# Inner products read from ScalarE's copy, r3 ahead of r7, and the next layer's statistics and logits rearranged in a two-layer graph kernel

## The chip, the cores and the metric

The kernel runs on one core of one Trainium2 chip. The metric is the device time of one execution in microseconds (us); the median of three runs is given. One further execution was taken with the hardware profiler, and every duration below that has a place in the timeline comes from it. PE is TensorE (matrix products), ACT is ScalarE, DVE is VectorE, POOL is GpSimd, and SP issues the DMAs.

## The reference

Sixteen batches of x (1024 nodes by 512 features) pass through two residual layers with one adjacency matrix adj (1024 by 1024). All is float32.

```python
# layer 0
h = relu(layernorm(x))
x = x + (adj @ h) @ W0 + bias
# layer 1
h = relu(layernorm(x))
u = h @ W                              # 512 x 512
s1, s2 = u @ a1, u @ a2                # one number per node each
e = leaky_relu(s1[:, :, None] + s2[:, None, :], 0.2) * adj
att = softmax(e, axis=2)
x = x + elu(att @ u + beta * u)
```

In the kernel, u is the name of the normalized and rectified input of layer 1 (the reference's second h), so that s1 = u . (W a1) and s2 = u . (W a2): two dot products per node with vectors v that are worked out once. These dot products are called the logits.

## The kernel before

**Products.** Each large product of a batch is done as seven half-size products and sums (Strassen's scheme in Winograd's form). Layer 0's adj @ h has p1, p2, p6, p5, p7, p3 and p4, in that order. Their results are added up in PSUM banks Y, W and X (two banks each, p = 0 and 1) and read from there into C11, C12, C22, C21 and the sums S1, S2, S4, in SBUF. Its product with W0 (`po`) has seven products again. Layer 1 has the products `z` (attention by u) and `pq` (by W).

**The second level.** For batches 1 to 15 the function `products_a2` (line 215) takes each of p1 to p4 apart once more: `inner_steps(prod)` returns seven inner products r1 to r7 as steps. An inner product is two matmul calls, which are four records in the trace. r1, r6 and r7 are accumulated in a PSUM tile that the product has for itself, `yx` (its left half is y; the right half, x, is used where the bank isn't being started): r1 writes y, ScalarE copies that value to `t[:, 0]`; r6 adds to y, VectorE adds that and `t5` (ScalarE's copy of r5) into `t[:, 1]`; r7 adds to y again, ScalarE copies it to `t[:, 2]`. Then VectorE adds `t[:, 0:2]` to bank 1 behind r3, and what r7 gave to bank 0. The pool of `yx` has two buffers, so p6 takes that of p1, p5 that of p2, p7 that of p6, and so on: a product's r1 waits until all readers of y of the product two before it are done. Names in the trace: `y_p1y` is y of p1, `y_p1t` is its t, `in_p` are the sums of parts of h that a product's inner products take as inputs, `y_Y`, `y_W` and `y_X` are the banks, `y_C` the blocks C, `y_S` the sums and also the scratch tile for statistics.

Two products are interleaved (p1 with p2, p6 with p5, p7 with p3), two inner products to a numbered step; p4 is interleaved with the first product by W0. Steps 0 to 6 are p1 and p2, 7 to 13 p6 and p5, 14 to 20 p7 and p3, 21 to 27 p4. `reads` folds a finished bank into its blocks C.

**The side work.** After each numbered step, `after(k)` issues the work that a plan has put there. All engines keep the order in which the program issues their instructions (the wrapper at line 118 sees to it, which is why every record has that line). There is no scheduler: an instruction that waits holds all that is behind it on its engine.

`plan_out` (line 1093) is such a plan, for the output of layer 0 of the batch before. That output lies in four tiles xr, named by (half, quarter): (0,0), (0,1), (1,0), (1,1), two chunks of 128 nodes each. For each tile: `keep` stores it, `stats` takes the mean and the variance, `relu` normalizes it in place (ScalarE), `logits` takes the dot products with both v (VectorE, two reductions a chunk), `store` writes u to DRAM. `inner_left` makes sums of parts of adj @ h's inputs (VectorE), `load_res` loads the next residual tiles, `begin` puts the bias into a bank.

Statistics have two forms in the class `Norm` (line 454). `sums(k)` works on ScalarE, two passes over a chunk with accumulated sums and one small scaling; the last chunk is followed by three small GpSimd instructions (scale, power -1/2, product) that give `r` and `nb`, the factor and the offset of the relu. `stats()` works on VectorE, one bn_stats and one bn_aggr a chunk, followed by four small GpSimd instructions.

**The last batch.** Batch 15 has no next batch to prepare. In its layer 0 stands the softmax of layer 1's first batch instead: `FIRST_A` (line 1163) and `FIRST_B` (line 1167) say at which step. R reloads a masked row block from DRAM (`er<-ed`, SP) into a buffer of the pool b4 (12 buffers, shared with t, C and the sums), E takes its exponentials (ScalarE, four instructions with accumulated sums), V transposes it (VectorE, two), S and s spread the sums, B and b take the SBUF tiles for the transposed halves, D, d and T divide out the sums on the diagonal and add blocks for the product. Steps of `FIRST_A` lie in steps 0 to 27 of the batch, those of `FIRST_B` in the rest.

```python
order = "r1 r4 r5 r6 r2 r7 r3" if first else "r1 r2 r5 r4 r6 r3 r7"
turns = ones[0:2] + [t for m in range(5) for t in (twos[m], ones[m + 2])] + twos[5:]
for m in range(7):
    turns[2 * m]()
    turns[2 * m + 1]()
    if m == 0:
        for prod, p in behind:
            reads(prod, p)
    elif m in (4, 5):
        reads(one, halves[m - 4])
    after(k + m)
```

Of the kernel before, what the change touches and what calls it, by code (L numbers as in the profile page):

```python
# [65 lines left out]
def kernel(  # L66
# [12 lines left out]
    B, N, D = x.shape  # L79
# [21 lines left out]
    def bank(name):  # L101
        return psum.tile([P, 512], F32, tag="ps", name=name)
# [21 lines left out]
    def add(o, i0, i1, op=ALU.add):  # L124
        dve.tensor_tensor(o, i0, i1, op=op)
# [89 lines left out]
    def products_a2(name, inner, weighted, after, s4):  # L215


        read = ReadA(name, None, s4)
        read.s3_now = False
        banks = {}  # L220
        by_name = {p[0]: (n, *p[1:]) for n, p in enumerate(PRODUCTS)}

        def inner_steps(prod):

            _, an, bn, kind, first, last = by_name[prod]
            left, sums, right, ext = inner[prod]
            if first:
                banks[kind, 0], banks[kind, 1] = bank(f"{name}_{kind}0"), bank(f"{name}_{kind}1")  # L230
            i0, i1 = banks[kind, 0], banks[kind, 1]
            yx = psum_y.tile([P, 512], F32, tag="psy", name=f"{name}_{prod}y")
            y, x = yx[:, 0:256], (i0 if first else yx)[:, 256:512]
            t = b4.tile([P, 4, 256], F32, tag="b4", name=f"{name}_{prod}t")
            t5 = sums[:, 3].rearrange("p c d -> p (c d)")
            lefts = {
                "r1": left[:, 0:2, P : 2 * P], "r2": left[:, 2:4, P : 2 * P],
                "r7": left[:, 0:2, 0:P], "r4": left[:, 2:4, 0:P], "r5": sums[:, 0],
                "r6": sums[:, 1], "r3": sums[:, 2],
            }  # L240
            rights = {
                "r1": right[:, 0:2, 0:256], "r7": right[:, 0:2, 256:512],
                "r2": right[:, 2:4, 0:256], "r3": right[:, 2:4, 256:512],
                "r5": ext[0], "r6": ext[1], "r4": ext[2],
            }
            outs = {
                "r1": (y, True), "r4": (i0[:, 0:256], first), "r5": (x, False),
                "r6": (y, False), "r7": (y, False), "r2": (i1[:, 0:256], first),
                "r3": (i1[:, 256:512], False),
            }  # L250

            def step(r):
                o, start = outs[r]
                for k in range(2):
                    pe.matmul(
                        o, lefts[r][:, k, :], rights[r][:, k, :], start=(start and k == 0),
                        stop=(k == 1), skip_group_check=True,
                    )
                if r == "r1":
                    act.copy(t[:, 0, :], y)  # L260
                elif r == "r5":
                    act.copy(t5, x)
                elif r == "r6":
                    add(t[:, 1, :], y, t5)
                elif r == "r7":
                    act.copy(t[:, 2, :], y)
                    if first:
                        i0v = i0.rearrange("p (a n) -> p a n", a=2)
                        add(i0v, i0v, t[:, 2:3, :].to_broadcast([P, 2, 256]))
                    else:  # L270
                        add(t[:, 3, :], y, t5)
                        add(out(0), i0, t[:, 2:4, :].rearrange("p a n -> p (a n)"))
                elif r == "r3":
                    add(out(1), i1, t[:, 0:2, :].rearrange("p a n -> p (a n)"))

            def out(p):
                return read.block("C21", p) if prod == "p4" else banks[kind, p]

            order = "r1 r4 r5 r6 r2 r7 r3" if first else "r1 r2 r5 r4 r6 r3 r7"
            return [partial(step, r) for r in order.split()]  # L280

        def reads(prod, p):
            read(prod, p, banks[by_name[prod][3], p])

        k = 0
        behind = []
        for one, two in (("p1", "p2"), ("p6", "p5"), ("p7", "p3")):
            ones, twos = inner_steps(one), inner_steps(two)
            halves = (0, 1) if one == "p1" else (1, 0)
            turns = ones[0:2] + [t for m in range(5) for t in (twos[m], ones[m + 2])] + twos[5:]  # L290
            for m in range(7):
                turns[2 * m]()
                turns[2 * m + 1]()
                if m == 0:
                    for prod, p in behind:
                        reads(prod, p)
                elif m in (4, 5):
                    reads(one, halves[m - 4])
                after(k + m)
            behind = [(two, p) for p in ((1, 0) if two == "p3" else (0, 1))]  # L300
            k += 7
        inn = inner_steps("p4")
        steps = iter(weighted.steps(0, read.c["C11"]))
        for m in range(7):
            inn[m]()
# [3 lines that stand above are left out]
            elif m > 4:  # L309
                read.last(6 - m)  # L310
            next(steps)()
            if m == 3:
                next(steps)()
            elif m == 6:
                read.s3(0)
                read.s3(1)
            after(k + m)
        return read.left()

    class Weighted:  # L320
# [17 lines left out]
        def steps(self, n, left):  # L338

            prod, _, bn, kind, first, last = self.products[n]  # L340
            first = first and (kind, 0) not in self.banks

            def step(q, i, dc):
                if first and i == 0 and dc == 0:
                    self.banks[kind, q] = bank(f"{self.name}_{kind}{q}")
                ps = self.banks[kind, q].rearrange("p (i o) -> p i o", i=2)
                pe.matmul(
                    ps[:, i, :], left[:, dc, ts(2 * q + i, P)], self.w[:, W_BLOCK[bn], dc, :],
                    start=(first and i == 0 and dc == 0), stop=(last and dc == 1),
                    skip_group_check=True,  # L350
                )
                if i and dc:
                    self.done(prod, q, ps)

            return [partial(step, q, i, dc) for q in range(2) for i in range(2) for dc in range(2)]
# [93 lines left out]
    def stats(mv, src):  # L449
        st = stat.tile([P, 6], F32, tag="bn", name="bn")  # L450
        dve.bn_stats(st, src)
        dve.bn_aggr(mv, st)
# [145 lines left out]
    def junk(k):  # L598

        return junks[-1][:, k, :]  # L600
# [7 lines left out]
    class LayerOut:  # L608
# [17 lines left out]
            xr = xrs[self.b, nh, q]  # L626
            sp.dma_start(out=x1d[self.b][nh, q], in_=xr.rearrange("p k d -> p (k d)"))

        def stats(self, nh, q, k):
            xr = xrs[self.b, nh, q]  # L630
            if k == 0:
                self.us[nh, q] = xr
                self.norms[nh, q] = Norm(f"u{self.b}_{nh}_{q}", xr, junk(0))
            self.norms[nh, q].sums(k)

        def relu(self, nh, q):
            self.norms[nh, q].relu()
# [378 lines left out]
    halves = [(nh, q) for nh in range(2) for q in range(2)]  # L1016
# [76 lines left out]
    def plan_out(o, b):  # L1093

        return steps(
            (-1, o.keep, 0, 1), (-1, o.keep, 1, 0), (-1, o.keep, 1, 1), (0, o.stats, 0, 1, 0),
            (1, o.relu, 0, 0), (2, o.stats, 1, 0, 0), (3, o.stats, 1, 0, 1),
            (4, o.stats, 0, 1, 1), (6, o.relu, 1, 0), (7, o.relu, 0, 1), (8, o.stats, 1, 1, 0),
            (9, o.stats, 1, 1, 1), (11, o.relu, 1, 1),
            (3, o.store, 0, 0), (7, o.store, 1, 0), (8, o.store, 0, 1), (13, o.store, 1, 1),  # L1100
            (2, o.logits, 0, 0, 0), (3, o.logits, 0, 0, 1), (7, o.logits, 1, 0, 0),
            (8, o.logits, 1, 0, 1), (9, o.logits, 0, 1, 0), (10, inner_left, b, "p7"),
            (11, o.logits, 0, 1, 1), (12, inner_left, b, "p3"), (13, o.logits, 1, 1, 0),
            (14, o.logits, 1, 1, 1), (15, inner_left, b, "p4"), (16, o.store_logits),
            (18, begin, b, "Y"), (24, begin, b, "X"),
            (9, load_res, b, 0, 0), (12, load_res, b, 0, 1), (15, load_res, b, 1, 0),
            (18, load_res, b, 1, 1),
        )

# [15 lines left out]
    def plan_softmax(order, s):  # L1125
# [35 lines left out]
        13: {9: "N n"},  # L1161
    }
    FIRST_A = {
        13: "R0", 15: "B E0", 16: "V0 R1", 17: "E1", 18: "V1 R2", 19: "E2", 20: "V2 b", 21: "R3",
        23: "E3", 24: "V3 R4 S", 25: "E4", 26: "V4 R5",
    }
    FIRST_B = {
        2: "E5 R6", 3: "V5 E6 R7", 4: "V6", 5: "E7", 6: "V7 s D", 7: "T1a", 8: "T1b", 11: "d T2a",
        12: "T2b",
    }  # L1170
    LOADS_U = {5: ("U00",), 7: ("U01",), 9: ("U10", "U11")}

# [115 lines left out]
```

## Time and profile before

| | |
|---|---|
| median of three runs | 2312.18 us (2311.99 to 2313.05) |
| profiled execution | 2311.76 us |
| its span, first to last instruction | 2310.0 us |
| mean granted TensorE clock | 0.996 |
| chain that ended last, by engine | PE 56%, DVE 21%, ACT 13%, DMA 4%, issue 4% |
| layer 0 of one batch: batches 1 to 5 | 68.76 us |
| batches 6 to 14 | 69.31 us |
| batch 15 | 81.35 us |
| layer 1 of one batch | 72.24 us |

The lengths of batches are taken from the start of one batch's first p1 record to the next one's, and in layer 1 from `z` to `z`. A record of the timeline reads: start in us from the span's start, length in us, engine, line, operation, output <- inputs, size, number of neighbouring records of the same kind drawn together, and in brackets how long the engine stood idle ahead of it and whose end let it go on. In the list of waits, a row names the waiting instruction, the one waited for, and the total in us, the number of times and the longest.

### The profile page before, as it was taken

To read this page: it belongs to the slowest core of one execution; us is meant where nothing else is said; L and a number is where in the kernel's file an instruction comes from. 1 tells how busy PE (TensorE), PEld (TensorE's weight loads), DVE (VectorE), ACT (ScalarE), POOL (GpSimd) and SP (SyncE) were. 2 spreads that over 40 slices of the span, in tenths; PEclk is the share of its full clock that TensorE was granted. 3 is DMA by queue.
4 is the path that set the end of the run, shared out by engine and by line. 5 is a ranking of instruction groups with operands and counts; after the bars stand their busy time and mean duration, and the time that the engine had idled before them with its cause. 6 is when DMAs were issued, how large, how long until landed. Compare 5 with 4: busy or idle time off the path is not lost.

```text
span 2310.0 us, 29805 instructions
## 1 busy us (share of the span) xinstructions
PE 2262.2 (98%) x8524; PEld 1608.5 (70%) x8524; DVE 1894.6 (82%) x4225; ACT 1585.9 (69%) x4256; POOL 372.1 (16%) x553
## 2 busy tenths in 40 slices
PE   9999999999999999999899999999999999999998
PEld 5788888888888888888665566655665556655565
DVE  7888888888888888888788888888887888878774
ACT  3776777776777776776466677677776777767753
POOL 1111111111111111111011222112221122201220
PEclk9999999999999999999999999999999999999999
DMA  7333454433444433343545544554446543455441
GB/s 216 126 128 124 142 167 129 143 122 128 139 156 137 141 124 128 120 146 123 191 133 166 161 136 164 189 170 150 144 161 195 169 133 125 142 184 165 132 129 37
DMA packets 194294, 336.04 MB, mean 145 GB/s; under 512 B 78801, under 2 KB 86993, under 8 KB 194129
## 3 DMA queue, kind: packets, MB, share of 16 engines
q1 hardware_dynamic: 193808, 333.61, 44.4%
q8 instruction: 67, 1.10, 0.2%
q14 instruction: 99, 0.80, 0.1%
q10 hardware_dynamic: 320, 0.52, 0.1%
HBM read 228.33 MB, written 109.91 MB: 146 GB/s over the span
## 4 chain that ended last, share of the span: by engine, by line
PE 56%; DVE 21%; ACT 13%; DMA 4%; issue 4%; SPq 1%; POOL 1%; DVEq 0%; ACTq 0%
PE z_Y L118 14%; PE pq_Y L118 8%; PE z_X L118 7%; ACT y_S L118 5%; PE pq_X L118 4%; PE y_Y L118 4%; PE z_W L118 4%; DVE in_p L118 4%; PE po_Y L118 3%; PE y_X L118 2%; DVE y_S L118 2%; DVE hS L118 2%; PE y_p4y L118 2%; DVE xr L118 2%; PE pq_W L118 2%
## 5 line engine op out<-in xcount | busy, mean ns | idle before, releaser
L118 POOL TENSOR_TENSOR x<-x,r 128x512 f32<-128x512 f32 x120 | 198.7, 1673 | 935.0 <-DVE x L118 325.6
L118 ACT ACTIVATE e<-e,nm 128x256 f32<-128x256 f32 x480 | 237.1, 497 | 140.7 <-DVE nm L118 140.7
L118 DVE CUSTOM_DVE_ANT_0 e<-e,mask 128x256 f32<-128x256 f32 x512 | 215.4, 476 | 106.9 <-DMA mask<-maskd 89.7
L118 PE MATMUL z_Y<-pT,ul_U 128*128 128x512 f32 x512 | 224.9, 592 | 0.0
L118 ACT ACTIVATE e<-s2b,s1b 128x256 f32<-128x256 f32 x512 | 216.4, 500 | 0.0
L118 PE MATMUL po_Y<-w_c,y_C 128*128 128x256 f32 x768 | 189.2, 380 | 1.1 <-DVE xr L118 1.1
L118 PEld LDWEIGHTS z_Y<-pT,ul_U 128*128 128x128 f32 x512 | 97.3, 190 | 115.6 <-issue 108.1
L118 PE MATMUL pq_Y<-w_c,z_C 128*128 128x256 f32 x768 | 174.5, 380 | 0.7 <-ACT z L118 0.6
L118 DVE CUSTOM_DVE_ANT_0 y_S<-xr,v_bc 128x512 f32<-128x512 f32 x240 | 165.3, 689 | 11.5 <-ACT y_S L118 0.5
L118 PEld LDWEIGHTS pq_Y<-w_c,z_C 128*128 128x128 f32 x768 | 145.5, 190 | 28.9 <-issue 7.7
L118 PEld LDWEIGHTS po_Y<-w_c,y_C 128*128 128x128 f32 x768 | 146.0, 191 | 22.7 <-DVE xr L118 2.3
L118 DVE STREAM_TRANSPOSE pT<-e 128x512 f32<-128x512 f32 x240 | 155.5, 686 | 1.0
L118 ACT ACTIVATE y_S<-xr 128x512 f32<-128x512 f32 x120 | 75.8, 631 | 92.3 <-DVE xr L118 91.3
L118 ACT ACTIVATE h<-h,nb_h,r_h 128x512 f32<-128x512 f32 (+1 forms) x132 | 98.2, 792 | 54.5 <-POOL nb_h L118 54.5
L118 PE MATMUL po_X<-w_c,y_S 128*128 128x256 f32 x512 | 115.7, 379 | 0.0
L118 PE MATMUL pq_X<-w_c,z_S 128*128 128x256 f32 x512 | 115.6, 379 | 0.0
L118 PE MATMUL z_Y<-pT_T,ul_U 128*128 128x512 f32 x256 | 113.6, 594 | 1.2 <-DVE pT_T L118 1.1
L118 PE MATMUL z_X<-pT,ul_S 128*128 128x512 f32 x256 | 112.5, 592 | 0.0
L118 PE MATMUL z_Y<-pT_T,ul_S 128*128 128x512 f32 x256 | 112.5, 592 | 0.0
L118 PE MATMUL z_W<-pT,ul_U 128*128 128x512 f32 x256 | 112.5, 592 | 0.0
L118 PE MATMUL z_X<-pT_T,ul_S 128*128 128x512 f32 x256 | 112.5, 592 | 0.0
L118 PEld LDWEIGHTS po_X<-w_c,y_S 128*128 128x128 f32 x512 | 97.3, 190 | 13.2
(231 smaller groups left out, 5113.3 us busy)
## 6 DMA issues: line engine op xcount, KB each, us to landing
mask<-maskd SPq DMA_DIRECT2D x128, 512.0 KB
h<-in_x_dram SPq DMA_DIRECT2D x64, 512.0 KB
xr<-in_x_dram SPq DMA_DIRECT2D x256, 128.0 KB
x1d<-xr SPq DMA_DIRECT2D x64, 512.0 KB
ul_U<-ud_U SPq DMA_DIRECT2D x64, 512.0 KB
x<-x1d SPq DMA_DIRECT2D x64, 512.0 KB
out_dram<-x SPq DMA_DIRECT2D x252, 128.0 KB
ud_U<-xr SPq DMA_DIRECT2D x60, 512.0 KB
```

Of the source, the lines that this page charges most:

```text
L118: return lambda *args, **kwargs: tc.keep_in_program_order(f(*args, **kwargs))
```

## The change

It has six parts. (1) Where a bank isn't being started, VectorE's sum behind r7 takes r7's result from ScalarE's copy `t[:, 2]` and no longer from y in PSUM. (2) The order of inner products of a product that starts its bank (p1, p2, p5) becomes r1 r4 r5 r2 r6 r3 r7. (3) The reads of the first product of a pair move from steps 4 and 5 to steps 5 and 6, bank 1 first, and so stand behind the copies of r7. (4) Statistics of the tile (0,1) are taken with `stats()` on VectorE, at step 0, and no longer with two calls of `sums` at steps 0 and 4. (5) `plan_out` is rearranged: relu(0,0) from step 1 to 0, relu(0,1) from 7 to 2, logits of (0,1) from 9 and 11 to 3 and 4, those of (0,0) from 2 and 3 to 1 and 2, stats of (1,0) and (1,1) one to three steps sooner, sums for p3 and p4 one and three steps later; two stores and two loads move too. (6) The softmax in batch 15 starts with a reload at step -1, and its exponentials E0 to E3 are spread over steps 4 to 23; E4 moves into the rest of the batch.

```diff
--- before.py
+++ after.py
@@ -268,7 +268,7 @@
                         i0v = i0.rearrange("p (a n) -> p a n", a=2)
                         add(i0v, i0v, t[:, 2:3, :].to_broadcast([P, 2, 256]))
                     else:
-                        add(t[:, 3, :], y, t5)
+                        add(t[:, 3, :], t[:, 2, :], t5)
                         add(out(0), i0, t[:, 2:4, :].rearrange("p a n -> p (a n)"))
                 elif r == "r3":
                     add(out(1), i1, t[:, 0:2, :].rearrange("p a n -> p (a n)"))
@@ -276,7 +276,7 @@
             def out(p):
                 return read.block("C21", p) if prod == "p4" else banks[kind, p]
 
-            order = "r1 r4 r5 r6 r2 r7 r3" if first else "r1 r2 r5 r4 r6 r3 r7"
+            order = "r1 r4 r5 r2 r6 r3 r7" if first else "r1 r2 r5 r4 r6 r3 r7"
             return [partial(step, r) for r in order.split()]
 
         def reads(prod, p):
@@ -286,7 +286,6 @@
         behind = []
         for one, two in (("p1", "p2"), ("p6", "p5"), ("p7", "p3")):
             ones, twos = inner_steps(one), inner_steps(two)
-            halves = (0, 1) if one == "p1" else (1, 0)
             turns = ones[0:2] + [t for m in range(5) for t in (twos[m], ones[m + 2])] + twos[5:]
             for m in range(7):
                 turns[2 * m]()
@@ -294,10 +293,10 @@
                 if m == 0:
                     for prod, p in behind:
                         reads(prod, p)
-                elif m in (4, 5):
-                    reads(one, halves[m - 4])
+                elif m > 4:
+                    reads(one, 6 - m)
                 after(k + m)
-            behind = [(two, p) for p in ((1, 0) if two == "p3" else (0, 1))]
+            behind = [(two, 1), (two, 0)]
             k += 7
         inn = inner_steps("p4")
         steps = iter(weighted.steps(0, read.c["C11"]))
@@ -626,12 +625,16 @@
             xr = xrs[self.b, nh, q]
             sp.dma_start(out=x1d[self.b][nh, q], in_=xr.rearrange("p k d -> p (k d)"))
 
-        def stats(self, nh, q, k):
+        def stats(self, nh, q, k=None):
+
             xr = xrs[self.b, nh, q]
-            if k == 0:
+            if not k:
                 self.us[nh, q] = xr
                 self.norms[nh, q] = Norm(f"u{self.b}_{nh}_{q}", xr, junk(0))
-            self.norms[nh, q].sums(k)
+            if k is None:
+                self.norms[nh, q].stats()
+            else:
+                self.norms[nh, q].sums(k)
 
         def relu(self, nh, q):
             self.norms[nh, q].relu()
@@ -1093,17 +1096,16 @@
     def plan_out(o, b):
 
         return steps(
-            (-1, o.keep, 0, 1), (-1, o.keep, 1, 0), (-1, o.keep, 1, 1), (0, o.stats, 0, 1, 0),
-            (1, o.relu, 0, 0), (2, o.stats, 1, 0, 0), (3, o.stats, 1, 0, 1),
-            (4, o.stats, 0, 1, 1), (6, o.relu, 1, 0), (7, o.relu, 0, 1), (8, o.stats, 1, 1, 0),
-            (9, o.stats, 1, 1, 1), (11, o.relu, 1, 1),
-            (3, o.store, 0, 0), (7, o.store, 1, 0), (8, o.store, 0, 1), (13, o.store, 1, 1),
-            (2, o.logits, 0, 0, 0), (3, o.logits, 0, 0, 1), (7, o.logits, 1, 0, 0),
-            (8, o.logits, 1, 0, 1), (9, o.logits, 0, 1, 0), (10, inner_left, b, "p7"),
-            (11, o.logits, 0, 1, 1), (12, inner_left, b, "p3"), (13, o.logits, 1, 1, 0),
-            (14, o.logits, 1, 1, 1), (15, inner_left, b, "p4"), (16, o.store_logits),
+            (-1, o.keep, 0, 1), (-1, o.keep, 1, 0), (-1, o.keep, 1, 1), (0, o.stats, 0, 1),
+            (0, o.relu, 0, 0), (1, o.stats, 1, 0, 0), (2, o.relu, 0, 1), (3, o.stats, 1, 0, 1),
+            (5, o.relu, 1, 0), (6, o.stats, 1, 1, 0), (8, o.stats, 1, 1, 1), (10, o.relu, 1, 1),
+            (1, o.logits, 0, 0, 0), (2, o.logits, 0, 0, 1), (3, o.logits, 0, 1, 0),
+            (4, o.logits, 0, 1, 1), (7, o.logits, 1, 0, 0), (9, o.logits, 1, 0, 1),
+            (10, inner_left, b, "p7"), (13, inner_left, b, "p3"), (15, o.logits, 1, 1, 0),
+            (16, o.logits, 1, 1, 1), (16, o.store_logits), (18, inner_left, b, "p4"),
+            (3, o.store, 0, 0), (5, o.store, 0, 1), (8, o.store, 1, 0), (13, o.store, 1, 1),
             (18, begin, b, "Y"), (24, begin, b, "X"),
-            (9, load_res, b, 0, 0), (12, load_res, b, 0, 1), (15, load_res, b, 1, 0),
+            (8, load_res, b, 0, 0), (10, load_res, b, 0, 1), (14, load_res, b, 1, 0),
             (18, load_res, b, 1, 1),
         )
 
@@ -1161,12 +1163,12 @@
         13: {9: "N n"},
     }
     FIRST_A = {
-        13: "R0", 15: "B E0", 16: "V0 R1", 17: "E1", 18: "V1 R2", 19: "E2", 20: "V2 b", 21: "R3",
-        23: "E3", 24: "V3 R4 S", 25: "E4", 26: "V4 R5",
+        -1: "R0", 4: "E0", 8: "B V0 R1", 10: "E1", 12: "V1 R2", 17: "E2", 18: "V2 R3", 23: "E3",
+        25: "b", 26: "V3 R4 R5",
     }
     FIRST_B = {
-        2: "E5 R6", 3: "V5 E6 R7", 4: "V6", 5: "E7", 6: "V7 s D", 7: "T1a", 8: "T1b", 11: "d T2a",
-        12: "T2b",
+        2: "E4 S R6", 3: "V4 E5 R7", 4: "V5 E6", 5: "D V6 E7", 6: "V7 s", 7: "T1a", 8: "T1b",
+        11: "d T2a", 12: "T2b",
     }
     LOADS_U = {5: ("U00",), 7: ("U01",), 9: ("U10", "U11")}
 
```

## The prediction

> **What bounds the kernel now.** I read, in this order, the share of each engine and of each engine on the chain that ended last, the waits of TensorE, two windows of one batch each, and TensorE's timeline with its idle gaps.
>
> ```profile
> PE 2262.2 (98%) x8524; PEld 1608.5 (70%) x8524; DVE 1894.6 (82%) x4225; ACT 1585.9 (69%) x4256; POOL 372.1 (16%) x553
> ...
> PE y_p7y L118 <- DVE y_p6t L118: 16.7, 15, 1.4
> PE y_p3y L118 <- DVE y_p3t L118: 5.2, 1, 5.2
> PE y_X L118 <- ACT y_C L118: 4.3, 15, 0.3
> PE y_Y L118 <- ACT y_C L118: 3.5, 9, 0.4
> PE y_p4y L118 <- DVE y_p4t L118: 2.1, 1, 2.1
> ```
>
> [...]TensorE is never short of work for long; all that the change can win in the fifteen batches of this stage is in these five rows, about 32 us, and anything it makes late by a microsecond per batch costs about 15. The windows of batch 8 and batch 15 (length, then busy time of PE, PEld, DVE, ACT, POOL):
>
> ```profile
> 573.62:642.93 69.31, 67.55 (x309) 58.10 (x308) 58.48 (x132) 50.98 (x132) 10.20 (x25) 1.00 0.43 138
> 1058.83:1140.18 81.35, 71.57 (x309) 59.80 (x308) 63.01 (x136) 44.60 (x138) 4.67 (x13) 0.96 0.47 155
> ```
>
> [...]No other engine is full, so losses are moments at which one instruction on VectorE or ScalarE stands in a queue while TensorE needs its result. These moments are:
>
> ```profile
> 587.12 1.13 PE L118 MATMUL y_Y<-adjT_T,hS 128*128 128x256 f32 x4 [0.38 <-ACT y_C L118]
> ...
> 599.92 1.13 PE L118 MATMUL y_p7y<-adjT_B,h 128*128 128x256 f32 x4 [1.09 <-DVE y_p6t L118]
> ...
> 603.93 1.13 PE L118 MATMUL y_X<-adjT_B,hS 128*128 128x256 f32 x4 [0.29 <-ACT y_C L118]
> ...
> 1101.84 2.07 PE L118 MATMUL y_p3y<-adjT_B,hS 128*128 128x256 f32 x4 [5.22 <-DVE y_p3t L118]
> ...
> 1116.18 1.13 PE L118 MATMUL y_p4y<-adjT_T,h 128*128 128x256 f32 x4 [2.08 <-DVE y_p4t L118]
> ```
>
> An inner product (four records) takes 0.864 us from start to start, and a wait costs 0.10 more, because the group after it takes 1.13 where others take 1.03. By starts, batch 8 loses 0.65 at y_Y, 0.22 at y_p6y (hidden in its start, 589.06), 1.36 at y_p7y, 0.56 at y_X and 0.05 in p4: 2.84. So a batch with no such loss would take 69.31 - 2.84, about 66.5.
>
> **What the Trainium skill says.** "GPSIMD Engine Reference", section Key points: GpSimd "Shares its SBUF interfaces with VectorE — contention with DVE instructions in a 2-port perf mode or with two SBUF inputs." The trace agrees, and gives the size. Unheld, then beside VectorE's sums of two SBUF tiles:
>
> ```profile
> 583.37 0.19 POOL L118 TENSOR_SCALAR r_u<-mv_u 128x2 f32<-128x2 f32 x1 [6.04 <-ACT y_S L118]
> 583.64 0.70 POOL L118 TENSOR_TENSOR r_u<-r_u,half 128x2 f32<-128x2 f32 x1
> 584.42 0.20 POOL L118 TENSOR_TENSOR nb_u<-mv_u,r_u 128x2 f32<-128x2 f32 x1
> ...
> 632.37 0.74 POOL L118 TENSOR_SCALAR r_h<-mv_h 128x2 f32<-128x2 f32 x1 [5.16 <-ACT y_S L118]
> 633.19 1.02 POOL L118 TENSOR_TENSOR r_h<-r_h,half 128x2 f32<-128x2 f32 x1
> ...
> 632.37 0.69 DVE L118 TENSOR_TENSOR hS<-hS,h 128x512 f32<-128x512 f32 x1
> ```
>
> The 0.19 us step became 0.74: it ended with the sum beside it. I read this as a rule for the working: a GpSimd instruction that meets a two-input VectorE instruction ends no sooner than that one. "TensorE: Matmul & The Clock Gate", Part 1, says that the clock halves after an idle window of about 3.4 us. The trace agrees: the group behind the 5.22 us wait took 2.07, those behind waits of 1 or 2 us 1.13. No other page bears on the argument.
>
> **The change, part by part.** Times t count from the start of p1 in batch 8 (573.62); turn n starts at 0.864 n if nothing waits (turn 11 at 583.12 does). The order that the change gives was laid out engine by engine, with durations from the trace.
>
> *The copies.* r7 reads y from ScalarE's copy, so y is free once the copy is made, and VectorE's add leaves the wait of p7 on p6's y: saves the 1.36. C11's and C12's copies go behind r7's copies, so they no longer hold ScalarE when y is due; r3 in front of r7 gives i1 sooner. Together the y_X, the y_Y and the 1.36 go: about 2.6 of the 2.84. The add costs the same: a sum of 256 columns takes 0.42 with y from PSUM (y_p1t, 579.07) and with both inputs in SBUF (in_p, 575.07). Free by itself.
>
> *Statistics of u(0,1).* ScalarE loses two chunks of 1.84 us each (574.90, 576.87: two passes, two reads, a scaling). VectorE gets bn_stats and bn_aggr twice, 0.79 a chunk start to start by the late chunks of layer 1:
>
> ```profile
> 1278.63 0.68 DVE L118 BATCH_NORM_STATS2 bn<-late 128x6 f32<-128x512 f32 x1
> 1279.35 0.18 DVE L118 BATCH_NORM_AGGREGATE mv_u<-bn 128x2 f32<-128x6 f32 x1
> ```
>
> GpSimd gets four small instructions in place of three (0.27 + 0.78 + 0.27 + 0.20 = 1.52 unheld). These stand at step 0 of p1, on VectorE behind the sums for the next inputs, whose last is issued at 577.81: t = 4.53 to 6.23 for the statistics.
>
> *Logits sooner.* Behind the statistics on VectorE come logits(0,0), four reductions, 2.91 us (579.42 to 582.33 in before), t = 6.11 to 9.02, then p1's r6 add to 9.36, then logits(0,1), which needs relu(0,1), which needs GpSimd's four steps, which start at t = 6.32 — beside logits(0,0), whose reductions each have two SBUF inputs. In flight they are 6.11-6.79, 6.83-7.52, 7.67-8.36 and 8.41-9.10. By the rule above GpSimd's steps end at 6.84, 8.07, 8.41 and 9.15 rather than 7.85. The relu's first half then runs on ScalarE 9.18 to 9.99, logits(0,1) from 10.02: two reductions 1.35, the Y add 0.60, two reductions 1.40, and only then p2's r6 add, from 13.4 to 13.84. That add frees y for p2's r7, in turn 13, planned for 11.23. TensorE resumes at 13.9: a loss of 2.6. Bounds: with GpSimd unheld 13.14, a loss of 1.9 here; with every step held to the end of a reduction begun later, one reduction (0.74) more. I take the middle.
>
> *What is late next.* ScalarE had the relus of 1.52 us in front of p6's copy; now relu(1,0) stands behind a GpSimd chain of the same kind, then C11's copies, p2's copy and 1.71 us of statistics of (1,1) come before p6's first copy, which ends at t = 18.7 to 18.9. p6's r5, turn 17, planned at 14.69, starts at 18.7 to 19.0: both delays together 4.0 to 4.3 with the restarts of 0.10. Then about 0.1 to 0.3 at p3's r7 (behind the four sums for p4, now in step 18) and about 0.2 in p4: 4.6 to 4.9 a batch, against 2.84. Net +1.75 to +2.05; I take +1.9, for each of 14 batches: +26.6.
>
> *Loads and stores.* Two stores change places and the loads of residuals come a step sooner; SP issues them, each in tenths of a microsecond, and what they fetch is used tens of microseconds later. Nothing, unless a buffer comes free later; then SP stands, and load_res with it.
>
> *Batch 15.* It alone has the softmax's exponentials for layer 1 (reload a row block, four exponentials, transposes). In before they are packed into p3 and p4, and each reload waits for a buffer:
>
> ```profile
> 1098.06 0.51 ACT L118 ACTIVATE er<-er,nm 128x256 f32<-128x256 f32 x1 [6.22 <-DMA er<-ed]
> ```
>
> That is where ScalarE stood, p3's add came late, TensorE idled 5.22 and then ran at half clock: 5.39 for the wait, 3.04 for the half clock, 2.34 at y_p4y, and 1.77 at the beginning of the rest of the batch: 12.5 of the 81.35. The change starts the reloads two thirds of a batch sooner, at step -1, one at a time. The buffer is then asked for before the exponentials want it, and I leave the 1.77 at its end, where the last exponentials still stand, as it is: 69.3 + 1.9 + 1.7 = 72.9, so -8.5. Bounds: nothing gained if the sooner reloads hold a buffer that p1 needs (above: 0), and 10.4 gained if the delays of the other batches are absent here (69.3 + 1.7).
>
> Sum: 26.6 - 8.5 = +18.1 on the profiled execution's 2311.76 (span 2310.0 and 1.8 around it): 2329.9. The median of the runs stands 0.4 above it, 2312.18: 2330.
>
> **The rivals.** *GpSimd isn't held by reductions*: the profile shows the hold beside sums, and beside a reduction only once (a GpSimd sum of 512 columns at 1282.97, in layer 1). Then logits(0,1) begins 1.3 sooner, p2's loss is 1.9 or less and ScalarE's chain after it too, a batch costs +0.3 to +0.5, batch 15 gives 10 back: 14 x 0.5 - 10 = -3, 2309. Against it: 632.37. *The other side: the change does what it says.* If p2's r6 add is done by t = 11.2 (the point that decides; it needs logits(0,1) begun by t = 7.4, or that add in front of it), the 2.6 are won, little comes back: -2.3 x 14 - 8.5 = -41, 2271. Against it: relu(0,1) can't start before GpSimd's chain, 7.85 at best. *Batch 15 gives nothing*, since the reload for E0 takes a buffer that the inner sums want and TensorE idles there instead, or ScalarE's lateness reaches one turn further (0.7 a batch): 2338 to 2340; for it, the buffers were the limit before, against it, the reloads are spread.
>
> **How the numbers follow.** Forecast 0.68 (2322 to 2338 by the bounds of +1.4 to +2.4 a batch); GpSimd unheld 0.12, mostly within no change; as intended 0.04; nothing from batch 15, or deeper, 0.12; others 0.04. A measurement of this kernel can tell 0.2%, 4.6 us, from none. Faster 0.08 (as intended, a third of the unheld case), same 0.09, slower 0.83. The range, 2308 to 2342, takes in the unheld case and the worse one.
>
> **What would show it.** Right: among TensorE's waits y_p7y for VectorE and y_X for ScalarE are gone, and new ones stand fifteen times, p2's y for VectorE's p2 copy at 2 to 3 us and p6's y for ScalarE at 1 to 1.5; GpSimd's four steps at p1 take 2.5 to 3 us and not 1.5; a batch takes about 71.2, batch 15 about 73. Wrong: no wait over 1 us in p2, batches under 69, or batch 15 still over 78; the first two say that the logits are hidden, the third that reloads still wait for a buffer.

## The result and the profile after

| | before | after |
|---|---|---|
| median | 2312.09 us (2311.33 to 2313.05, four runs) | 2328.69 us (2326.92 to 2329.89, four runs) |
| profiled execution | 2311.76 us | 2329.89 us |
| its span | 2310.0 us | 2328.1 us |
| layer 0, batches 1 to 5 | 68.76 us | 70.4 to 70.7 us |
| batches 6 to 14 | 69.31 us | 71.1 us |
| batch 15 | 81.35 us | 72.26 us |
| layer 1, all batches | 1169.8 us | 1172.8 us |

The ratio of the runs is 1.0071 (95% interval 1.0054 to 1.0088): slower by 0.7%. Of the 18.1 us between the spans, batches 1 to 14 give +24.5 (from the first p1 of batch 1 to that of batch 15: 967.90 before, 992.36 after), batch 15 gives -9.1, layer 1 gives +3.0 and what lies ahead of batch 1 gives -0.3. Layer 1 has the same instructions in both, and in the thirteen profiled executions of this study it took from 1169.4 to 1175.8 in no visible relation to what was edited, so its 3.0 are not counted as the change's.

TensorE's waits after the change (instruction, what it waits for, total us, times, longest):

```profile
PE y_p2y L118 <- DVE y_p2t L118: 31.9, 15, 2.3
PE y_p6y L118 <- ACT y_p6t L118: 11.7, 9, 1.3
...
PE y_p3y L118 <- DVE y_p3t L118: 1.2, 1, 1.2
```

All five rows shown of before have gone or, for p3, shrunk from 5.2 to 1.2. Two others stand in their place, and they are larger. (The waits named y_Y, z_Y and pq_Y that the full list has besides belong to the start of the kernel and to layer 1.) The windows of batch 8 and batch 15, in the columns used for before:

```profile
585.13:656.30 71.17, 68.86 (x309) 59.34 (x308) 59.96 (x136) 48.38 (x122) 12.66 (x26) 0.98 0.41 134
1083.01:1155.27 72.26, 67.81 (x309) 58.08 (x308) 64.61 (x143) 41.71 (x128) 6.66 (x14) 1.00 0.54 175
```

VectorE is 1.5 us busier in batch 8 and ScalarE 2.6 us less. Neither is near full, and yet the batch is 1.86 us longer: it is a matter of order. The chain can be read in the timeline of batch 8 (which begins at 585.13), here on GpSimd and VectorE:

```profile
591.50 0.54 POOL L118 TENSOR_SCALAR r_u<-mv_u 128x2 f32<-128x2 f32 x1 [2.67 <-DVE mv_u L118]
592.12 1.15 POOL L118 TENSOR_TENSOR r_u<-r_u,half 128x2 f32<-128x2 f32 x1
593.34 0.28 POOL L118 TENSOR_SCALAR nb_u<-mv_u 128x2 f32<-128x2 f32 x1
593.70 0.65 POOL L118 TENSOR_TENSOR nb_u<-nb_u,r_u 128x2 f32<-128x2 f32 x1
...
593.61 0.69 DVE L118 CUSTOM_DVE_ANT_0 y_S<-xr,v_bc 128x512 f32<-128x512 f32 x1
```

The last of the four small steps ends at 594.35, 0.05 us after the reduction of logits(0,0) that started at 593.61 and ended at 594.30; unheld such a step takes 0.20. Then ScalarE, VectorE and TensorE go on from one to the next:

```profile
594.39 1.52 ACT L118 ACTIVATE xr<-xr,nb_u,r_u 128x512 f32<-128x512 f32 x2 [1.84 <-POOL nb_u L118]
...
595.24 0.69 DVE L118 CUSTOM_DVE_ANT_0 y_S<-xr,v_bc 128x512 f32<-128x512 f32 x1 [0.59 <-ACT xr L118]
...
598.53 0.42 DVE L118 TENSOR_TENSOR y_p2t<-y_p2y,in_p 128x256 f32<-128x256 f32 x1
...
599.00 1.15 PE L118 MATMUL y_p2y<-adjT_B,h 128*128 128x256 f32 x4 [2.31 <-DVE y_p2t L118]
```

The brackets say who released whom: GpSimd the relu, the relu the logits of (0,1); the sum at 598.53 has no bracket, because VectorE was not idle. It had merely stood behind these logits, so the list of waits, which names the sum, doesn't name the instructions that made it late.

In batch 15 the waits of 5.2 and 2.1 us are gone. E0 to E3, which are now spread over steps 4 to 23, don't wait for their reloads: the record of E2 has no bracket, where E1 of before has 6.22 us. In before ScalarE waited for a reload five times in this batch, 19.7 us in all; now it does so twice, 3.4 in all, for exponentials in the rest of the batch, and TensorE's list of waits shows no loss from it:

```profile
1118.04 0.51 ACT L118 ACTIVATE er<-er,nm 128x256 f32<-128x256 f32 x1
...
1142.10 0.51 ACT L118 ACTIVATE er<-er,nm 128x256 f32<-128x256 f32 x1 [2.85 <-DMA er<-ed]
```

### The profile page after: what moved, and what is told of

It is laid out like the page before. It is cut to its first block, busy times and chain, and to the rows that moved or that the text cites. A ratio compares the mean times of both kernels' runs of the same rounds, so it can differ in the third digit from the quotient of the medians.

```text
span 2328.1 us, 29746 instructions
## 1 busy us (share of the span) xinstructions
PE 2264.6 (97%) x8524; PEld 1614.1 (69%) x8524; DVE 1916.3 (82%) x4285; ACT 1544.9 (66%) x4106; POOL 408.8 (18%) x568
## 4 chain that ended last, share of the span: by engine, by line
PE 62%; DVE 16%; ACT 10%; DMA 5%; POOL 3%; issue 3%; SPq 1%; DVEq 0%; ACTq 0%; POOLq 0%
PE z_Y L118 13%; PE pq_Y L118 7%; PE z_X L118 6%; PE y_Y L118 6%; PE y_X L118 4%; PE pq_X L118 4%; PE po_Y L118 4%; PE z_W L118 4%; ACT e L118 3%; DVE in_p L118 3%; ACT y_S L118 3%; PE y_p3y L118 2%; DVE xr L118 2%; DVE hS L118 2%; PE y_p4y L118 2%
## 5 line engine op out<-in xcount | busy, mean ns | idle before, releaser
L118 ACT ACTIVATE xr<-xr,nb_u,r_u 128x512 f32<-128x512 f32 x120 | 91.1, 806 | 70.8 <-POOL nb_u L118 70.8
L118 ACT ACTIVATE y_S<-xr 128x512 f32<-128x512 f32 x90 | 56.8, 632 | 91.8 <-DVE xr L118 91.4
```

Source lines behind the costliest of these rows:

```text
L118: return lambda *args, **kwargs: tc.keep_in_program_order(f(*args, **kwargs))
```

## The experiments

Each was timed beside the kernel before, and the ratios are to it. Its median lay between 2312.09 and 2313.83 us in these timings, so that a difference between two of the other kernels is good to about 2 us. Where a stretch at half clock follows a wait in some batches only, the last section says which.

**The logits of (0,1) behind p2's sum.** The changed kernel with

```diff
-(3, o.logits, 0, 1, 0), (4, o.logits, 0, 1, 1),
+(5, o.logits, 0, 1, 0), (6, o.logits, 0, 1, 1),
```

> The changed kernel, with the logits of (0,1) moved from steps 3 and 4 to steps 5 and 6, so that p2's r6 sum stands in front of them on VectorE. Theory M (two queues are late because of the same relu chain: VectorE in front of p2's r7, ScalarE in front of p6's r5, and the second deadline holds the whole delay): the wait of p2 is gone, a wait of p6's y for ScalarE's copy of 3.5 to 4 us takes its place in every batch, a batch stays at 70.3 to 71.1, time 2322 to 2329, or more if TensorE drops to half clock behind so long a gap. Rival R1 (VectorE's queue alone is the loss): p2's 2.3 us come back, a batch takes 68.3 to 68.8, time 2293 to 2298.

Measured: 2337.12 us, ratio 1.010 (1.0085 to 1.0115), 7 to 8 us slower than the changed kernel. TensorE's waits:

```profile
PE y_p6y L118 <- ACT y_p6t L118: 18.4, 14, 1.3
PE y_p5y L118 <- ACT y_p2t L118: 16.7, 14, 1.2
PE y_p6y L118 <- ACT y_p1t L118: 5.6, 11, 2.1
```

The largest wait of the changed kernel is gone and nothing is won: ScalarE's lateness, which it had covered, comes to light in three waits within 7 us. It isn't the one wait of 3.5 to 4 us that was expected, as p2's r7 copy and p1's are late too. Batches 6 to 14 take 70.9 or 72.5 us by turns, and the timeline of one of the longer shows why:

```profile
677.36 1.13 PE L118 MATMUL y_p5y<-adjT_T,hS 128*128 128x256 f32 x4 [1.19 <-ACT y_p2t L118]
...
679.81 2.08 PE L118 MATMUL y_p6y<-ext,in_p 128*128 128x256 f32 x4 [1.31 <-ACT y_p6t L118]
681.67 1.72 PE L118 MATMUL y_X<-ext,hS 128*128 128x256 f32 x4
```

In place of 1.13 and 1.03 us these two groups took 2.08 and 1.72: TensorE ran at half clock for a while, in 7 of the 14 batches. R1 is refuted: even where the clock stayed full, batches took 70.2 and 70.9, not 68.3 to 68.8. Theory M holds, with the half clock that it left open.

**ScalarE's relu and statistics later too.** The same, and

```diff
-(5, o.relu, 1, 0), (6, o.stats, 1, 1, 0), (8, o.stats, 1, 1, 1), (10, o.relu, 1, 1),
+(7, o.relu, 1, 0), (8, o.stats, 1, 1, 0), (9, o.stats, 1, 1, 1), (11, o.relu, 1, 1),
```

> The changed kernel, with the logits of (0,1) at steps 5 and 6 and also ScalarE's relu(1,0) and the statistics of (1,1) two steps later (relu(1,0) 5 to 7, statistics 6 to 8 and 8 to 9, relu(1,1) 10 to 11), so that both queues give way to TensorE's needs. Theory M: both waits shrink, a batch takes 67.8 to 68.5, time 2286 to 2293. R1: no more than the run with the logits alone would give, 2293 to 2298. R2 (the bn statistics on VectorE are the loss): no gain, 2325 to 2330.

Measured: 2285.47 us, ratio 0.9881 (0.9865 to 0.9898); batches of 67.4 (1 to 5) and 68.1 (6 to 14). Both waits have gone from the list. One of the three that the first experiment brought to light is left, and it is that experiment's in number and size:

```profile
PE y_p6y L118 <- ACT y_p1t L118: 5.6, 11, 2.1
```

What the first edit could not win at all, the two together win: some 43 us against the changed kernel. The bn statistics are still on VectorE here, which speaks against R2. This is still 12.5 us more than the changed kernel with the plan of before (below); which of the plan's other moves cost that was not tried apart.

**ScalarE's part alone.** The changed kernel, the logits left at steps 3 and 4, with

```diff
-(5, o.relu, 1, 0), (6, o.stats, 1, 1, 0),
+(6, o.relu, 1, 0), (7, o.stats, 1, 1, 0),
```

> The changed kernel, with relu(1,0) at step 6 in place of 5 and the first statistics of (1,1) at step 7 in place of 6, so that p6's first copy stands in front of them on ScalarE; the logits stay at steps 3 and 4. Theory M: p2's wait of about 2 us stays, the wait of p6's y for ScalarE goes, a batch takes 69.4 to 70.1, time 2308 to 2314. R1 (VectorE's queue alone): nothing, 2326 to 2331.

Measured: 2321.25 us, ratio 1.004 (1.0026 to 1.0055): 7 us won, not 15 to 21. p6's wait is gone as expected, and where TensorE kept its clock a batch took 69.1 (batches 3 to 5) or 69.8 (6 to 14), the first better than expected, the second as expected. Others of 6 to 14 took 71.2. One of each, from the timeline:

```profile
453.93 1.13 PE L118 MATMUL y_p2y<-adjT_B,h 128*128 128x256 f32 x4 [2.31 <-DVE y_p2t L118]
...
523.75 1.34 PE L118 MATMUL y_p2y<-adjT_B,h 128*128 128x256 f32 x4 [2.31 <-DVE y_p2t L118]
524.89 1.91 PE L118 MATMUL y_p6y<-adjT_T,hS 128*128 128x256 f32 x4
526.60 1.70 PE L118 MATMUL y_Y<-adjT_T,hS 128*128 128x256 f32 x4
```

The wait is the same 2.31 us; behind the second, 1.4 us more go to the half clock. In the changed kernel 6 of the 9 waits of that length are followed by half clock too, and cost nothing further, because p6's copy is late in any case: the batches with it and without it all take 71.1 to 71.2.

**The plan of before.** The changed kernel with `plan_out` and `LayerOut.stats` of before:

```diff
-(-1, o.keep, 1, 1), (0, o.stats, 0, 1), (0, o.relu, 0, 0), ...
+(-1, o.keep, 1, 1), (0, o.stats, 0, 1, 0), (1, o.relu, 0, 0), ...
```

> The changed kernel with the plan and the statistics of before: only the copy, the order of inner products, the later reads and the new softmax steps of batch 15 remain. Theory M (all of the loss is in the plan): p7's, X's and Y's waits stay gone and no p2 wait appears, a batch takes 67.1 to 67.3 and batch 15 about 71, time 2272 to 2279. Rival R3 (the new order of inner products itself makes late what was early): a batch over 69, time over 2300.

Measured: 2272.97 us, ratio 0.9825 (0.9811 to 0.984); every batch from 1 to 14 takes 67.1 us, batch 15 takes 70.33. So the copy, the order, the later reads and the new softmax steps are worth 41 us against before, and the new plan with its statistics costs some 56 us on top of them. R3 is refuted.

**The statistics back on ScalarE.** The changed kernel with

```diff
-(0, o.stats, 0, 1),
+(0, o.stats, 0, 1, 0), (0, o.stats, 0, 1, 1),
```

> The changed kernel with the statistics of (0,1) back on ScalarE, both chunks at step 0; all else as changed. Theory M (the plan's order is the loss, not where the statistics are taken): the chain to relu(0,1) is about as long, through two chunks of 1.84 us on ScalarE, a batch takes 70.8 to 71.8, time 2326 to 2338. R2 (bn_stats on VectorE and the GpSimd chain behind it are the loss): a batch under 70, time under 2315.

Measured: 2331.73 us, ratio 1.0083 (1.0068 to 1.0099), batches of 70.5 and 71.2 to 71.4. No gain: to move the statistics back wins nothing of that 56 us. p2's wait is still there, 15 times, up to 2.0 us. GpSimd's chain is over 7.39 us into batch 8 here, but ScalarE, with two more chunks in front of it, comes to relu(0,1) at 9.44, against 9.26 in the changed kernel: the other of the relu's two conditions is then the later one. R2 as it was stated, a batch under 70 when the statistics go back, is refuted. (Both chunks stand at step 0 here, not at steps 0 and 4 as in before; that placing was not tried in the new plan.)

**One SBUF input in place of two.** The changed kernel; `logits` does for (0,0), and leaves out for good,

```diff
+            if (nh, q) == (0, 0):
+                for _ in v_bcs:
+                    dve.bn_stats(junk(1)[:, 0:6], self.us[nh, q][:, k, :])
+                return
```

> The changed kernel; the logits of (0,0) are left out, and in place of their four reductions VectorE runs four bn_stats on the same data, of nearly the same length (0.66 against 0.69) but with one SBUF input and no accumulator read. Theory H (two-input reductions hold GpSimd's steps): the chain behind the statistics of (0,1) takes 1.5 to 1.6 us in place of 2.85, relu(0,1) starts 1.3 us sooner, a batch takes 69.1 to 69.8, time 2303 to 2310. Rival (GpSimd's steps are slow for another reason, as their width or a busy queue): the chain stays at 2.6 us or more, and the gain is no more than VectorE's 0.2 to 0.3 us a batch, 2323 to 2327.

Measured: 2312.56 us, ratio 1.0001 (0.9993 to 1.001), 16 us faster than the changed kernel and a little short of the expectation; batches of 69.3 and 70.0. GpSimd in batch 8:

```profile
583.61 0.19 POOL L118 TENSOR_SCALAR r_u<-mv_u 128x2 f32<-128x2 f32 x1 [2.62 <-DVE mv_u L118]
583.88 0.69 POOL L118 TENSOR_TENSOR r_u<-r_u,half 128x2 f32<-128x2 f32 x1
584.64 0.19 POOL L118 TENSOR_SCALAR nb_u<-mv_u 128x2 f32<-128x2 f32 x1
584.92 0.20 POOL L118 TENSOR_TENSOR nb_u<-nb_u,r_u 128x2 f32<-128x2 f32 x1
...
588.72 0.55 POOL L118 TENSOR_SCALAR r_u<-mv_u 128x2 f32<-128x2 f32 x1 [3.60 <-ACT y_S L118]
589.35 1.16 POOL L118 TENSOR_TENSOR r_u<-r_u,half 128x2 f32<-128x2 f32 x1
```

The chain takes 1.51 us, each step at the length it has when nothing is beside it; in the changed kernel it took 2.85. Theory H holds. That it is the two SBUF inputs and not another trait of the reductions, the thirteen traces show together. Take the 128x2 GpSimd steps other than the power step that begin while one VectorE instruction is under way with 0.3 us or more to go: beside a sum or reduction with both inputs in SBUF all 572 ended after it, by about 0.05 us; beside one with an input in PSUM, or with one SBUF input, none of 329 did, and they took 0.19 to 0.20 us.

Two things show why a part of the gain is missing. relu(0,1) starts 1.33 us sooner (7.93 us into batch 8, not 9.26), but logits(0,1) only 0.74 (9.37, not 10.11), because VectorE has p1's r6 sum in front of them until 9.45; p2's wait shrinks from 2.3 to 1.6. And the lower two lines above: the logits of (0,1), now earlier, hold the next chain, that of (1,0), in the same way. ScalarE's relu(1,0), ahead of which ScalarE stands idle for 1.44 us, starts 13.60 us into the batch, against 14.62 in the changed kernel: 1.02 sooner, which is about what a batch gains.

**The softmax of before in batch 15.** The changed kernel with `FIRST_A` and `FIRST_B` of before:

```diff
-        -1: "R0", 4: "E0", 8: "B V0 R1", 10: "E1", ...
+        13: "R0", 15: "B E0", 16: "V0 R1", 17: "E1", ...
```

> The changed kernel with the softmax steps of before in batch 15. M: batch 15 goes back to 80 to 82, the others stay at 71, time 2336 to 2339. Rival (batch 15's gain comes from the copies and the later reads): batch 15 stays under 76, time 2328 to 2333.

Measured: 2336.47 us, ratio 1.0097 (1.0081 to 1.0112); batch 15 takes 80.94, the others 70.4 and 71.1, as expected of M. 8.7 of the 9.1 us that batch 15 gained go with the new softmax steps.

**The copy alone, the later reads alone, the order alone.** The kernel before with one of

```diff
-                        add(t[:, 3, :], y, t5)
+                        add(t[:, 3, :], t[:, 2, :], t5)
```

> The kernel before, with nothing but the first part: the sum behind r7 reads ScalarE's copy. The forecast gave this part the 1.36 us of p7's wait. Theory R4 (the wait list is to be taken by its name: VectorE's sum alone holds y): 1.3 us a batch come back, time 2290 to 2295. Theory K (ScalarE's copy of r7 is itself late, because it stands behind the copy of C12, which waits for VectorE's bank sum, so that y comes free no sooner): no change, batches of 68.7 and 69.3, time 2310 to 2315, with p7's wait now named for ScalarE.

```diff
-                elif m in (4, 5):
-                    reads(one, halves[m - 4])
+                elif m > 4:
+                    reads(one, 6 - m)
...
-            behind = [(two, p) for p in ((1, 0) if two == "p3" else (0, 1))]
+            behind = [(two, 1), (two, 0)]
```

> The kernel before, with nothing but the third part: the reads of a finished bank one step later, behind the copies of r7. Theory K: this is the part that takes the waits of p7, X and Y away; a batch takes 66.9 to 67.3, time 2277 to 2284. Theory R4: p7's wait stays, since the sum still reads y in PSUM; 68.0 to 68.7 a batch, time 2295 to 2305.

```diff
-            order = "r1 r4 r5 r6 r2 r7 r3" if first else "r1 r2 r5 r4 r6 r3 r7"
+            order = "r1 r4 r5 r2 r6 r3 r7" if first else "r1 r2 r5 r4 r6 r3 r7"
```

> The kernel before with the second part alone: r3 in front of r7 where a bank is started. Theory K: the sum of bank 1 and with it C11's first copy come sooner, so the wait of y_Y (9 times, 0.4) goes or shrinks, p7's stays: 68.0 to 68.6 a batch, time 2298 to 2306. Rival: the order changes nothing that TensorE waits for, 2310 to 2315.

In the third of these, the read at step 4 takes p1's bank 0 before the sum behind r7 has been added to it, so that C11 lacks that part; the instructions are those of the reordered kernel, but one read waits for less than it should, so its time is no measure of what the order is worth in a kernel that computes the right sum. Measured: the copy alone 2314.95 us (ratio 1.0009, 1.0001 to 1.0018), the reads alone 2280.63 (0.9865, 0.985 to 0.988), the order alone 2302.55 (0.9957, 0.994 to 0.9973). With the copy alone TensorE's waits begin

```profile
PE y_p7y L118 <- ACT y_p6t L118: 9.8, 15, 0.9
PE y_X L118 <- ACT y_C L118: 5.9, 15, 0.4
```

p7's wait has the name that was expected and falls from 16.7 to 9.8 us, but X's, 4 us further on, rises from 4.3 to 5.9, a new loss of 0.25 a batch opens at p3, and batches 1 to 5 take 68.75 as before. ScalarE's copy of p6's r7 stands behind C12's first copy and a relu, and starts 25.4 us into batch 8 in both kernels; what X waits for follows from it. Theory K holds for the copy.

With the reads alone p7's and Y's waits aren't in the list, though the sum still reads y in PSUM, and X's is 2.1 us in place of 4.3; batches take 66.8 and 67.0, and batch 15 takes 78.75 with the softmax steps of before. Theory K holds here too, and R4 is refuted.

With the order alone batches take 68.1 and 68.6 and the time is in the expected range, but the waits aren't those that were expected. p7's was to stay and has gone with Y's, while X's is nearly three times what it was and one of p5 is new:

```profile
PE y_X L118 <- ACT y_C L118: 11.7, 15, 0.8
...
PE y_p5y L118 <- DVE y_p5t L118: 3.7, 10, 0.7
```

So the later reads and the order each take p7's wait off the list, though the sum goes on reading y in PSUM, and the copy, which the list points to, does not.

**Later reads and new softmax steps together.** The kernel before with these two parts only.

> The kernel before with two parts alone: the later reads and the new softmax steps of batch 15; copy, order of inner products, statistics and plan as before. If the two gains simply add: a batch of 66.8 to 67.1 from the run with the reads alone, batch 15 at 70 to 72, time 2268 to 2274. Rival (the order r3 in front of r7 is needed for batch 15's gain, or for the others): over 2276.

Measured: 2272.04 us, ratio 0.9823 (0.9808 to 0.9837), batches of 66.8 and 67.0, batch 15 at 71.03. The gains add, as expected. It is the fastest kernel here, though not told apart from the one with the copy and the order as well (2272.97): with the later reads and the new softmax steps in place, these two parts win nothing more. Both kernels beat the kernel before by 40 us and the changed one by some 56. Of batch 15, the new softmax steps take 7.7 us here (78.75 to 71.03).

## Why the prediction was right, and where it was not

*Time and sign.* Forecast 2330, measured 2328.69. The sum was 26.6 - 8.5 = +18.1 on the profiled execution; measured +24.5 - 9.1 for the two parts of layer 0, +15.4, and the rest, 2.7, from layer 1 and the start, which the change doesn't touch. So the agreement of the two 18.1 is in part luck; the medians differ by 16.6.

*GpSimd's chain and p2.* This was the step that carried the forecast, and it held in detail, in us from the start of batch 8: chain forecast 6.32 to 9.15, measured 6.37 to 9.22; relu 9.18, measured 9.26; logits(0,1) 10.02, measured 10.11; p2's sum 13.4, measured 13.40; TensorE goes on at 13.9, measured 13.87. The chain unheld was forecast at 1.52 and measured at 1.51. The rival of an unheld GpSimd is refuted.

*ScalarE and p6.* Forecast: p6's copy ends at 18.7 to 18.9, and TensorE starts p6's r5 at 18.7 to 19.0. Measured: 18.84 for the copy in batch 8 (603.62 and 0.35 us), where TensorE, made late by half clock until 18.26, starts p6's r5 at 19.12; 18.91 in batch 9, which kept its clock. That the two deadlines aren't added, but the later holds the delay, is what the first three experiments show: one edit alone gains nothing or 7 us, both gain 43. The sign that p6's wait stands fifteen times failed: it stands 9 times, because in the six batches with half clock TensorE came late to it by itself.

*A batch.* +1.9 forecast, 24.5 / 14 = 1.75 measured, inside the range that was given. The kernel with the plan of before shows the two terms apart: for batches 6 to 14 it takes 67.1, so 2.2 are won of the 2.84 of waits, and the plan puts 4.0 on top, where the forecast had 4.6 to 4.9. Both terms were some 0.6 to 0.9 too large, and the errors cancel. *Batch 15.* -8.5 forecast, -9.1 measured; 7.7 to 8.7 of it are part (6)'s, by what else is in the kernel. *Loads and stores.* Nothing was forecast, and no row of TensorE's waits names one in these batches.

*The step that failed.* The forecast of the time held, but one step of its sum did not. The prediction says of the copy: "y is free once the copy is made, and VectorE's add leaves the wait of p7 on p6's y: saves the 1.36". The copy alone saves nothing. The add was the last to release y by the list, but the copy it waited for was itself behind C12's copy, and X's turn behind it was late by the same queue. What takes p7's and Y's waits away and halves X's is the later reads (-31.6 us alone), which the prediction counted with the copy in one sum. The sum, 2.6 a batch, came out at 2.2 to 2.3 for batches 6 to 14 and 1.7 to 1.9 for 1 to 5; its division did not.

*A ceiling that was too low.* The five rows of waits, about 32 us, were said to be all that the change could win. The later reads and the new softmax steps win 40. The list counts only the time in which TensorE stood: the prediction itself has 0.10 for each restart and 3.04 us at half clock in batch 15, and these go with the waits.

*A reading that was too bold.* From a few cases the prediction took it that groups behind waits of 1 or 2 us start at 1.13, that is, at full clock. Behind waits of 1.8 to 2.3 us this was so only in some batches. That the half clock cost the changed kernel nothing, since p6's copy was late in any case, is luck for the forecast.

*A rival that was priced unevenly.* For a GpSimd that isn't held, the prediction has logits(0,1) 1.3 us sooner in one place and p2's loss only 0.7 smaller in another. The run with one SBUF input in place of two, which frees the chain, shows the second: 0.74 and 0.7.

*The other side.* The estimate for the case in which the change does what it says, 2271, is about what kernels with the plan of before reach, 2272 and 2273; the new plan itself, rearranged, was brought to 2285.

## What to carry to other kernels

On engines that keep program order, lay out each queue that has to serve TensorE with every instruction in front of the one that matters, and find the last deadline: the wait that the list puts first may only cover another, and to take it away alone can gain nothing. Move work that waits for another engine behind the short instruction that frees a buffer, not in front of it; here two short moves in the plan were worth some 43 us, and reads placed one step later 32. Don't put a chain of small GpSimd steps beside VectorE reductions of two SBUF tiles when something hangs on its end.

## What the runs showed of the hardware

TensorE's half clock comes with much shorter gaps than the 5.2 us of before. "TensorE: Matmul & The Clock Gate", Part 1, gives a window of about 3.4 us, free-running, and half clock after an idle one. The traces hold the granted clock as a record of its own, and agree on the length and on the free running: the six stretches at half clock in layer 0 of the changed kernel last 3.41 us each and begin at 456.62, 528.29, 599.98, 883.28, 954.96 and 1026.64, which is 21, 21, 83, 21 and 21 times 3.413 us from one to the next. They don't agree that the whole window has to be idle. Here are the two waits of 2.31 us that end at 599.00 and at 670.18, cut along these windows (start and end, length, busy time of PE with its records, granted clock, DMA share, GB/s):

```profile
596.57:599.98 3.41, 1.10 (x6) 1.00 0.40 161
599.98:603.39 3.41, 3.41 (x10) 0.50 0.40 143
...
668.24:671.66 3.42, 1.48 (x7) 1.00 0.29 116
671.66:675.07 3.41, 2.25 (x11) 1.00 0.52 180
```

The first wait lies in one window and leaves 2.31 us of it idle: the next window is at half clock. The second, just as long, is cut by a border and leaves 1.94 and, with a part of p6's wait, 1.16: full clock. Over layer 0, from batch 1 on, of all thirteen traces, 40 windows at full clock were idle for 1.95 us or more, and half clock followed all 40; of 3887 that were idle for less than 1.81, it followed none; of the 8 between, 3. The ends of matmuls are modelled in these traces, which may be why the limit isn't sharp.

This sorts the other cases too. With the logits later, the waits of 1.2 and 1.3 us brought half clock in the 7 of 14 batches in which they left 2.0 us or more of one window idle. The wait of 3.0 us at p3 of batch 15, with the softmax of before, brought none: a border cuts it, and leaves 1.53 and 1.51 us. So the measurement decides here: a gap well under 3.4 us can bring the half clock, gaps add up within a window, and whether one wait brings it depends on where it falls. Behind these short gaps the half clock cost 1.4 to 1.6 us a time, unless a later deadline covered it.

A GpSimd instruction beside VectorE's reductions of two SBUF tiles ended about 0.05 us after the reduction, or, the power step, 0.55 us after it (592.12 to 593.27, the reduction ending at 592.72): 1.15 us for 0.69.
